# Thirteen gathers of a graph layer fetched row by row by SyncE instead of by GpSimd's indirect DMA

## The chip, the core and the metric

The kernel runs on one core of a Trainium2 chip. Its five engines (TensorE for products, VectorE and ScalarE for elementwise work, GpSimd, and SyncE, which here only issues transfers) run side by side and wait for one another through semaphores. Transfers between the memory of the chip (HBM) and the core's working memory are issued by SyncE or GpSimd and carried by 16 transfer engines. The metric is the device time of one execution in microseconds; less is better.

## The reference

One residual block around two graph convolutions, N = 6250 nodes, E = 100000 edges sorted by destination, D = 512, all float32:

```python
def reference(x, src, dst, W1_0, W1_1, b1, gamma, beta, W2_0, W2_1, b2):
    h = relu(layernorm(x))
    deg  = segment_sum(1, src);  dinv = where(deg > 0, rsqrt(deg), 0)
    norm = -dinv[src] * dinv[dst]
    prop = lambda h: segment_sum(h[src] * norm[:, None], dst)
    t = h @ W1_0 + prop(h) @ W1_1 + b1
    t = layernorm(t) * gamma + beta;  t = where(t >= 0, t, 0.01 * t)
    return x + t @ W2_0 + prop(t) @ W2_1 + b2
```

So each of the two layers fetches, for each of 100000 edges, one row of 2 KB of a table and adds it to the row of the edge's destination.

## The kernel before

**Chunks and gathers.** The edges are cut into NC = 782 chunks of P = 128. For chunk t one `indirect_dma_start` on GpSimd (L250, L480, L490) fetches the 128 table rows named by column t of `sidx`, one row to each partition. The first 76 chunks of layer 0 (RAW) are fetched from `x` itself and are put through the layer norm in place; the later ones come from `tab[0]`, whose rows of W = 528 numbers carry the node's `dinv` in column 512 (so the rows need scaling after the gather), and in layer 1 from `tab[1]`, whose rows of 512 are already scaled. Layer 1's first 27 chunks (L490) are fetched before the last blocks of `tab[1]` are written, with the late rows held out and added by other means.

**Where the rows lie.** `places` is a buffer of 63 slots of 128 x 528 numbers. `slot(k)` gives the slot of chunk k (k counts on through layer 1): a ring of R = 55 slots, and in a first round also the 8 slots behind them. `lent` lends the weights' buffers to the first 12 chunks. From the middle of layer 0 on, the last 8 slots hold the second layer's weights (`w_late`, loaded by L896). `gather_to` (L473 to L483) issues gathers up to 55 chunks ahead of what has been summed.

**Groups of sums.** Three chunks are a unit, four units a group: NS = 66 groups a layer, 12 chunks each but for the first. `choose` (L589) builds on VectorE the matrices `sel` (128 edges x 32 nodes) that say which edge belongs to which node; `scale` (L636) multiplies them in layer 0 by the `dinv` column of the gathered rows (L647); `sums` (L652) multiplies them on TensorE with the rows (L660), and ScalarE copies the sum to `agg` (L673). The last chunk of a group is the last product of its sums.

**Blocks.** The 49 blocks of 128 nodes follow the groups. When all groups that reach into block i are summed, `turn` (L781) loads the block's own rows (`load_h`, L545; in layer 1 also `load_x`, L564), `place` (L685) moves the sums to their nodes (L693), `first_half` and `second` multiply with the two weights (L568), and `finish` (L746) adds the bias. In layer 0 it also does the layer norm, and SyncE stores the block twice: to `tab[1]` (L777, from `t`) and, after ScalarE and VectorE have made `g` (L779, L780; a single buffer), to `h_tab` (L782). In layer 1 SyncE stores the output (L757).

**Order.** The queues of TensorE, GpSimd and SyncE are in the order in which the program is written; VectorE's and ScalarE's are ordered by the framework's scheduler, by its own estimate of times. The loop over groups is at the end of `usual_path`: for each g it calls `gather_to`, finishes blocks, chooses, scales and sums. SyncE's transfers take eight semaphores in turn, so that a transfer also waits until the one eight places before it has landed. `general_path` runs only where the input is not of the expected form, which it is here.

Of the kernel before, what the change touches and what calls it, by code (L numbers as in the profile page):

```python
# [9 lines left out]
F32 = mybir.dt.float32  # L10
BF = mybir.dt.bfloat16
I32 = mybir.dt.int32
AF = mybir.ActivationFunctionType
OP = mybir.AluOpType
AX = mybir.AxisListType
# [3 lines left out]
SP = mybir.EngineType.SP  # L19

P = 128
# [4 lines left out]
Q = 32  # L26
NQ = P // Q
STEP = 3
DRIFT = 32
RE = 14  # L30
RAW = 76
PAD = 16
LATE = 3
AHEAD_OF = 27
JOIN = 12


def parts(r):
# [5 lines left out]
def gnn_kernel(  # L44
# [33 lines left out]
    nc = tc.nc  # L78
    N, D = x.shape
# [6 lines left out]
    NC = -(-E // P)  # L86
# [16 lines left out]
    tab = [dram.tile([n, w], F32, name=f"tab{i}") for i, (n, w) in enumerate(((NB * P, W), (N + 1, D)))]  # L103
    zero_row = (NB - LATE) * P
# [26 lines left out]
    pick = const.tile([P, P], BF, name="pick")  # L131
    src_lo = const.tile([P, P], BF, name="src_lo")
    src_hi = const.tile([P, RAW], F32, name="src_hi")
    p_id = const.tile([P, 1], F32, name="p_id")

# [288 lines left out]
    n_unseen = usual_path(tc, locals())  # L424
    stay.close()
    with tc.If(n_unseen > 0):
        general_path(tc, x, src, dst, bias1, bias2, gam, bet, w_sb, (W2_1, W2_0), dinv, ndinv, ident, iota_r,
                     eps, out)


def usual_path(tc, have):
    nc = tc.nc
    (x, out, tab, h_tab, ndinv, sidx, dlx, iota_r, w_sb, W2_1, W2_0, w_late, ident, eps, ones, first, nodes_ps, node_of, minus,
     unsorted, dinv, sdinv, bias1, bias2, gam, bet, unseen, unit, N, E, D, NB, NC, NU, NS, KD, rows, places, R,
     load_rest, sc, pick, src_lo, src_hi, eidx, e_src, zero_row, p_id, lent, X) = (
        have[n] for n in ("x out tab h_tab ndinv sidx dlx iota_r w_sb W2_1 W2_0 w_late ident eps ones first nodes_ps node_of "
                          "minus unsorted dinv sdinv bias1 bias2 gam bet unseen unit N E D NB NC NU NS KD rows places "
                          "R load_rest sc pick src_lo src_hi eidx e_src zero_row p_id lent X").split())
# [12 lines left out]
    with ExitStack() as es:  # L451
# [11 lines left out]

        LATER = places.shape[1] - R

        def slot(k):
            return k - X if k < X + R + LATER else (k - X - LATER) % R

        def zr(layer, t):
            k = layer * NC + t  # L470
            return lent[k] if k < X else places[:, slot(k), :D]

        def gather_to(layer, summed_to):  # L473
            nonlocal gathered
            end = summed_to + R
            if layer == 0:
                end = max(end, min(end + LATER, X + LATER + 2 * R))
            for t in range(gathered, min(end, NC)):
                own_scale = layer == 0 and t >= RAW
                nc.gpsimd.indirect_dma_start(  # L480
                    out=places[:, slot(t), :] if own_scale else zr(layer, t), out_offset=None,
                    in_=x if layer == 0 and t < RAW else tab[layer],
                    in_offset=bass.IndirectOffsetOnAxis(  # L483
                        ap=lidx[:, t - SHIFTED : t - SHIFTED + 1] if layer and t >= SHIFTED else sidx[:, t : t + 1], axis=0))
            gathered = max(gathered, min(end, NC))
# [149 lines left out]
        def scale(sel, chunk, of=(0, NQ)):  # L635

            at = chunk[0][0]
            start = max(chunk[of[0]][0], RAW)
            end = chunk[min(of[1], len(chunk)) - 1][-1] + 1
            if end <= start:  # L640
                return
            each = sel.rearrange("p q s e -> p (q s) e")
            cut = sorted({start, end} | {t for t in range(start + 1, end) if slot(t) != slot(t - 1) + 1})
            for lo, hi in zip(cut, cut[1:]):
                v = each[:, lo - at : hi - at, :]
                k = slot(lo)
                last = nc.vector.tensor_tensor(  # L647
                    v, v, places[:, k : k + hi - lo, D : D + 1].to_broadcast([P, hi - lo, Q]), op=OP.mult)
            return last

        def sums(layer, g, sel, chunk, cnt=None, some=None, opens=True, closes=True):

            n = len(chunk)
            if opens:
                summed[0] = psum.tile([P, D], F32, name="ps")
            ps = summed[0]
            if some is None:
                some = [(s, q) for s in range(STEP) for q in range(n) if s < len(chunk[q])]
            for s, q in some:
                nc.tensor.matmul(ps[q * Q : (q + 1) * Q, :], sel[:, q, s, :], zr(layer, chunk[q][s]), start=(s == 0),  # L660
                                 stop=(s == len(chunk[q]) - 1 and (cnt is None or chunk[q][0] >= AHEAD_OF)))
# [224 lines left out]
        for layer in range(2):  # L886
# [5 lines left out]
            for g in range(NS - 1):  # L892
                gather_to(layer, STEP * unit[g])
                if layer == 0 and g == NS // 2:
                    for k, w in enumerate((W2_1, W2_0)):
                        nc.sync.dma_start(w_late[:, k], w.rearrange("(k p) d -> p k d", p=P))  # L896
                if layer == 0:
                    look_up("hT_ps")
                    find("hT_ps")
                    assert looked >= min(RAW, STEP * unit[g + 1])  # L900
                due = []

                def finished():
# [17 lines left out]
                sel, chunk = chosen.pop(g) if g in chosen else choose(g)  # L921
                if layer == 0:
# [103 lines left out]
    return n_unseen  # L1026


def general_path(tc, x, src, dst, bias1, bias2, gam, bet, w_sb, w_late, dinv, ndinv, ident, iota_r, eps,
                 out):  # L1030


# [31 lines left out]
    z_tab = [dram.tile([N, D], F32, name=f"z_tab{i}") for i in range(2)]  # L1064
    e_src = dram.tile([NC, P], I32, name="e_src")
    e_dst = dram.tile([NC, P], I32, name="e_dst")
    w_sb = list(w_sb)
    for k, w in enumerate(w_late):
        w_sb.append(const.tile([P, KD, D], F32, name=f"w_late{k}"))
# [284 lines left out]
```

## Time and profile before

| | us |
|---|---|
| three timed runs, median (lowest to highest) | 2020.21 (2019.19 to 2025.29) |
| the profiled execution, its own time | 2021.09 |
| its span in the trace | 2019.3 |
| TensorE busy | 1669.7 (83%) |
| GpSimd busy | 1488.9 (74%) |
| VectorE busy | 707.6 (35%) |
| ScalarE busy | 414.3 (21%) |

The durations come from the one profiled execution, whose own time is 0.9 us above the median of the timed runs. A share of busy time is an average over the whole span; issuing of transfers by SyncE isn't counted as busy. SyncE's transfer issues are listed as SPq.

### The profile page before, as it was taken

What the parts mean: (1) busy time and instruction counts of PE and PEld (TensorE: products, weight loads), DVE (VectorE), ACT (ScalarE), POOL (GpSimd) and SP (SyncE); (2) the same over time, 40 slices, a digit from 0 to 9 for tenths busy, and PEclk for the clock granted to TensorE, in tenths of its full rate; (3) what the DMA queues carried; (4) which work ended last, traced back from release to release, by engine and by line L of the source; (5) the groups of instructions that cost most, each with busy time, mean ns of one, the idle gap of its engine ahead of it and who ended that gap; (6) DMA issues with size and microseconds to landing.
All of it is one profiled execution on the core that took longest, in us unless ns stands there. A gap on an engine that the chain in (4) does not pass through costs nothing.

```text
span 2019.3 us, 20097 instructions
## 1 busy us (share of the span) xinstructions
PE 1669.7 (83%) x6907; PEld 669.5 (33%) x6907; DVE 707.6 (35%) x1498; ACT 414.3 (21%) x752; POOL 1488.9 (74%) x1578
## 2 busy tenths in 40 slices
PE   5579998776887776888879888888888888888988
PEld 4444443222333222333323322323332223333333
DVE  7975554333354334343363111112221212222211
ACT  7895221111121111121111010011010001011100
POOL 6477777777777777777777777777777777777774
PEclk8789999888998888989999998889999989989999
DMA  9998888888988888888887787788787878788875
GB/s 329 396 374 269 267 269 263 249 258 245 303 265 253 251 260 241 267 266 260 245 261 241 245 257 247 247 252 255 240 255 246 254 244 257 241 263 251 272 235 171
DMA packets 190131, 528.41 MB, mean 262 GB/s; under 512 B 34652, under 2 KB 36426, under 8 KB 190020
## 3 DMA queue, kind: packets, MB, share of 16 engines
q0 software_dynamic: 125120, 415.88, 67.7%
q1 hardware_dynamic: 64860, 111.14, 15.2%
q8 instruction: 56, 0.92, 0.2%
q14 instruction: 55, 0.45, 0.1%
q10 hardware_dynamic: 40, 0.02, 0.0%
HBM read 475.25 MB, written 51.66 MB: 261 GB/s over the span
## 4 chain that ended last, share of the span: by engine, by line
PE 39%; DMA 31%; POOL 12%; issue 10%; DVE 5%; ACT 2%; POOLq 0%; DVEq 0%; SPq 0%; ACTq 0%
DMA places<-tab,sidx 24%; PE u_ps L568 16%; POOL places L480 12%; PE ps L660 12%; PE an_ps L693 7%; DMA places<-tab,lidx 5%; PE hT_ps L556 1%; PE hT_ps L803 1%; DVE hi L362 1%; DVE lo L362 1%; ACT places L539 1%; DMA dst_c<-in_dst_dram 1%; DMA tab<-places 1%; PE both_ps L379 1%; DVE sel L647 0%
## 5 line engine op out<-in xcount | busy, mean ns | idle before, releaser
L480 POOL DMA_INDIRECT places<-tab,sidx x1191 | 1130.5, 949 | 363.4 <-issue 256.2
L660 PE MATMUL ps<-places,sel 128*32 128x512 f32 x3104 | 517.1, 671 | 145.4 <-DMA places<-tab,sidx 81.9
L693 PE MATMUL an_ps<-agg,there 128*128 128x512 f32 (+1 forms) x554 | 270.0, 620 | 88.2 <-ACT agg L673 83.2
L480 POOL DMA_INDIRECT places<-tab,lidx x270 | 255.3, 946 | 82.3 <-issue 60.9
L660 PEld LDWEIGHTS ps<-places,sel 128*32 128x32 f32 x3104 | 103.1, 117 | 524.1 <-issue 190.0
L607 DVE TENSOR_TENSOR sel<-dlx,nodes_ps 128x384 f32<-128x384 f32 (+3 forms) x134 | 72.4, 541 | 415.1 <-PE ps L660 415.1
L568 PE MATMUL u_ps<-w,hT 128*128 128x512 f32 (+1 forms) x400 | 185.3, 607 | 20.6 <-ACT hT L558 20.1
L673 ACT ACTIVATE agg<-ps 128x512 f32<-128x512 f32 (+2 forms) x130 | 76.1, 587 | 570.1 <-PE ps L660 545.1
L568 PE MATMUL u_ps<-places,hT 128*128 128x512 f32 (+2 forms) x408 | 182.4, 591 | 2.9 <-ACT hT L558 2.9
L568 PE MATMUL u_ps<-w,aT 128*128 128x512 f32 x384 | 173.2, 594 | 2.7 <-DVE aT L805 2.7
L693 PEld LDWEIGHTS an_ps<-agg,there 128*128 128x128 f32 (+1 forms) x554 | 105.8, 199 | 209.6 <-issue 109.8
L568 PE MATMUL u_ps<-places,aT 128*128 128x512 f32 x384 | 173.5, 594 | 0.8 <-DVE aT L805 0.8
L647 DVE TENSOR_TENSOR sel<-sel,places 128x384 f32<-128x384 f32 (+11 forms) x71 | 34.4, 490 | 328.3 <-DMA places<-tab,sidx 323.2
L754 DVE TENSOR_TENSOR u_ps<-u_ps,bias 128x512 f32<-128x512 f32 x45 | 31.5, 700 | 281.8 <-PE u_ps L568 281.8
L558 ACT ACTIVATE hT<-hT_ps 128x512 f32<-128x512 f32 (+1 forms) x98 | 58.2, 594 | 278.1 <-PE hT_ps L556 277.6
L796 ACT ACTIVATE an<-an_ps,ndinv 128x512 f32<-128x512 f32 x96 | 65.8, 685 | 213.7 <-PE an_ps L693 213.5
L681 DVE TENSOR_SCALAR there<-iota_r,node_of 128x128 f32<-128x128 f32 (+1 forms) x286 | 85.8, 302 | 63.6 <-PE an_ps L693 61.3
L568 PEld LDWEIGHTS u_ps<-w,hT 128*128 128x128 f32 (+1 forms) x400 | 73.7, 195 | 96.5 <-issue 74.7
L766 ACT ACTIVATE sd<-mv,eps 128x1 f32<-128x1 f32 (+1 forms) x49 | 14.4, 294 | 433.5 <-DVE mv L764 433.5
L250 POOL DMA_INDIRECT places<-in_x_dram,sidx x63 | 60.0, 952 | 54.0 <-ACT junk L266 21.1
L568 PEld LDWEIGHTS u_ps<-places,hT 128*128 128x128 f32 (+1 forms) x408 | 74.4, 192 | 76.5 <-issue 71.5
L568 PEld LDWEIGHTS u_ps<-w,aT 128*128 128x128 f32 x384 | 70.7, 190 | 83.0 <-issue 77.8
(197 smaller groups left out, 1318.6 us busy)
## 6 DMA issues: line engine op xcount, KB each, us to landing
places<-tab,sidx POOLq DMA_INDIRECT x1191, 3.8
h_tab<-g SPq DMA_DIRECT2D x48, 256.0 KB
xt<-in_x_dram SPq DMA_DIRECT2D x48, 256.0 KB
out_dram<-t SPq DMA_DIRECT2D x48, 256.0 KB
tab<-t SPq DMA_DIRECT2D x46, 256.0 KB
tab<-places SPq DMA_DIRECT2D x22, 528.0 KB
h<-tab SPq DMA_DIRECT2D x45, 256.0 KB
h<-h_tab SPq DMA_DIRECT2D x45, 256.0 KB
```

Source lines behind the costliest of these rows:

```text
L250: nc.gpsimd.indirect_dma_start(out=lent[t] if t < X else places[:, t - X, :D], out_offset=None, in_=x, in_offset=bass.IndirectOffsetOnAxis ...
L362: nc.vector.tensor_tensor(t, s[:, g * 2 * GJ : (g + 1) * 2 * GJ].rearrange("p (j s) -> p j s", s=2)[:, :, None, :] .to_broadcast([EP, GJ, ...
L480: nc.gpsimd.indirect_dma_start(out=places[:, slot(t), :] if own_scale else zr(layer, t), out_offset=None, in_=x if layer == 0 and t < RAW ...
L558: nc.scalar.activation(hT[:, :, :r], ps[:, :, :r], AF.Copy)
L568: nc.tensor.matmul(u_ps[:r], hT[:, kc, :r], w[:, kc, :], start=(start and kc == 0), stop=(stop and kc == KD - 1))
L607: nc.vector.tensor_tensor(sel[:, q : q + k, :w, :], of, node[:, q : q + k, None, :].to_broadcast([P, k, w, Q]), op=OP.is_equal)
L647: last = nc.vector.tensor_tensor(v, v, places[:, k : k + hi - lo, D : D + 1].to_broadcast([P, hi - lo, Q]), op=OP.mult)
L660: nc.tensor.matmul(ps[q * Q : (q + 1) * Q, :], sel[:, q, s, :], zr(layer, chunk[q][s]), start=(s == 0), stop=(s == len(chunk[q]) - 1 and ( ...
L673: nc.scalar.activation(agg[g][: n * Q, lo : lo + w], ps[: n * Q, lo : lo + w], AF.Copy)
L681: behind[1] = nc.vector.tensor_scalar(t[:m, :r], iota_r[:m, :r], node_of[:m, g : g + 1], -(1.0 + i * P), op0=OP.subtract, op1=OP.is_equal)
L693: nc.tensor.matmul(placed[i][:r], t[:m, :r], agg[g][:m, :], start=(g == inside[i][0]), stop=(g == inside[i][-1]))
L796: nc.scalar.activation(an[:r], placed.pop(i)[:r], AF.Copy, scale=ndinv[:r, i : i + 1])
```

## The change

Six chunks of layer 0 (the last chunk of groups 17, 25, 33, 41, 49 and 57) and seven of layer 1 (of groups 12, 20, 28, 36, 44, 52 and 60) are no longer gathered by GpSimd. SyncE fetches their 128 rows one by one: each row is one transfer from the table at an address held in a register, in 16 pieces of 128 B (132 B in layer 0, so that the last piece brings column 512 along), written with gaps to 16 places of one partition. From group 7 in layer 0 and group 2 in layer 1 on, 8 rows are issued ahead of a group's work and 8 behind it; a chunk takes eight groups, and is summed two groups after the one that issued its last rows. The rows go to two slots of `places` in turn (the slots that held `W2_1`'s first half, whose load moves from group 33 to group 62), in layer 1 to the buffer of `W1_0`. The byte addresses are set up in group 6 by two loads of `src` and eight VectorE operations, in the memory of `pick` and `src_lo`, which are done by then; SyncE loads eight of them into registers ahead of each run of eight rows. Products with such a chunk read 16 pieces of 32 numbers; `scale` takes its chunk apart from its neighbours. `general_path` loads the first layer's weights again.

```diff
+AT_ONCE = 8
+PIECES = (16, 16)
+ONE_BY_ONE = (7, 2)
+SECOND = 32
...
+        for layer, g in enumerate(ONE_BY_ONE):
+            for j in range(SECOND):
+                at = g + -(-P * (j + 1) // (2 * AT_ONCE)) + 2
+                if at > NS - 5:
+                    break
+                t = STEP * unit[at + 1] - 1
+                one_by_one[layer * NC + t] = (layer * SECOND + j, R + j % 2 if layer == 0 else j % 2)
...
+        def set_starts():
+            for layer, some in enumerate(own_rows):
...
+                at, up = (pool.tile([P, D], F32, name="xt")[rows_of, :P] for _ in range(2))
+                nc.sync.dma_start(starts[rows_of], bass.AP(tensor=src.tensor, offset=src.offset + some[0] * P,
+                                                           ap=[[step * P, n], [1, P]]))
+                nc.vector.tensor_copy(at, starts[rows_of])
+                if layer:
+                    nc.vector.tensor_single_scalar(up, at, float(zero_row), op=OP.is_ge)
+                    nc.vector.tensor_add(at, at, up)
+                nc.vector.tensor_scalar_mul(at, at, 4.0 * tab[layer].shape[1])
+                nc.vector.tensor_copy(starts[rows_of], at)
...
+        def fetch(layer):
+            some = to_fetch[:AT_ONCE]
+            del to_fetch[:AT_ONCE]
+            for t in sorted({t for t, _ in some}):
+                fetch_rows(layer, t, [e for of, e in some if of == t])
+
+        def fetch_rows(layer, t, es):
...
+            _, regs = nc.values_load_multi_w_load_instructions(
+                starts[at : at + 1, e : e + n], engines=(SP,), ...)
+            flat = tab[layer].bitcast(U8).rearrange("n d -> (n d)")
+            w = PIECE[layer] + 1 - layer
+            flat = bass.AP(tensor=flat.tensor, offset=flat.offset,
+                           ap=[[1, flat.shape[0]], [PIECE[layer] * 4, PIECES[layer]], [1, w * 4]])
+            to = spread(layer * NC + t)[:, :, :w].bitcast(U8)
+            for j, start in enumerate(regs):
+                nc.sync.dma_start(to[e + j : e + j + 1], flat[bass.ds(start, 1)])
...
             for t in range(gathered, min(end, NC)):
+                if layer * NC + t in one_by_one:
+                    continue
...
                 if layer == 0 and g == NS // 2:
-                    for k, w in enumerate((W2_1, W2_0)):
-                        nc.sync.dma_start(w_late[:, k], w.rearrange("(k p) d -> p k d", p=P))
+                    nc.sync.dma_start(w_late[:, 1], W2_0.rearrange("(k p) d -> p k d", p=P))
+                if layer == 0 and g == NS - 4:
+                    nc.sync.dma_start(w_late[:, 0], W2_1.rearrange("(k p) d -> p k d", p=P))
...
+                if layer == 0 and g == ONE_BY_ONE[0] - 1:
+                    set_starts()
+                if g == ONE_BY_ONE[layer]:
+                    to_fetch.extend((t, e) for t in own_rows[layer] for e in range(P))
+                fetch(layer)
...
+                fetch(layer)
```

The first `fetch` of a group stands behind `gather_to` and ahead of the blocks' work, the second behind the group's sums.

More of the change, by code (lines that the diff above doesn't have):

```diff
@@ L12 @@
 I32 = mybir.dt.int32
+U8 = mybir.dt.uint8
 AF = mybir.ActivationFunctionType
@@ L130, in gnn_kernel @@
     sc = const.tile([P, 2, NB], F32, name="sc")
-    pick = const.tile([P, P], BF, name="pick")
-    src_lo = const.tile([P, P], BF, name="src_lo")
+    low_of = const.tile([P, 2, P], BF, name="low_of")
+    pick, src_lo = (low_of[:, k, :] for k in range(2))
+    starts = low_of.rearrange("p k e -> p (k e)").bitcast(I32)
     src_hi = const.tile([P, RAW], F32, name="src_hi")
@@ L464, in usual_path @@
         LATER = places.shape[1] - R
+        one_by_one, to_fetch = {}, []
+        for layer, g in enumerate(ONE_BY_ONE):
[5 more added lines that the diff above has]
+                one_by_one[layer * NC + t] = (layer * SECOND + j, R + j % 2 if layer == 0 else j % 2)
+        own_rows = [sorted(k - layer * NC for k in one_by_one if k // NC == layer) for layer in range(2)]
@@ new lines, in set_starts @@
+        def set_starts():
+            for layer, some in enumerate(own_rows):
+                n, step = len(some), some[1] - some[0]
+                assert some == [some[0] + j * step for j in range(n)]
+                rows_of = slice(layer * SECOND, layer * SECOND + n)
+                at, up = (pool.tile([P, D], F32, name="xt")[rows_of, :P] for _ in range(2))
[7 more added lines that the diff above has]
+                nc.vector.tensor_copy(starts[rows_of], at)
@@ new lines, in usual_path, with spread @@
+        PIECE = [D // k for k in PIECES]
+        w_free = w_sb[1].rearrange("p k d -> p (k d)")
+        def spread(k):
+            at = one_by_one[k][1]
+            row = places[:, at, :] if k < NC else w_free[:, at * W : (at + 1) * W]
+            return row.rearrange("p (a b) -> p a b", a=PIECES[k // NC])
+        def fetch(layer):
[3 more added lines that the diff above has]
+                fetch_rows(layer, t, [e for of, e in some if of == t])
@@ new lines, in fetch_rows @@
+        def fetch_rows(layer, t, es):
+            e, n = es[0], len(es)
+            at = one_by_one[layer * NC + t][0]
+            _, regs = nc.values_load_multi_w_load_instructions(
+                starts[at : at + 1, e : e + n], engines=(SP,), min_val=0, max_val=(tab[layer].shape[0] - 1) * tab[layer].shape[1] * 4,
+                skip_runtime_bounds_check_because="rows of the table")
+            flat = tab[layer].bitcast(U8).rearrange("n d -> (n d)")
[5 more added lines that the diff above has]
+                nc.sync.dma_start(to[e + j : e + j + 1], flat[bass.ds(start, 1)])
@@ L470, in zr @@
             k = layer * NC + t
+            if k in one_by_one:
+                return spread(k)[:, :, : PIECE[layer]]
             return lent[k] if k < X else places[:, slot(k), :D]
@@ L642, in scale @@
             each = sel.rearrange("p q s e -> p (q s) e")
-            cut = sorted({start, end} | {t for t in range(start + 1, end) if slot(t) != slot(t - 1) + 1})
+            cut = sorted({start, end} | {t for t in range(start + 1, end) if slot(t) != slot(t - 1) + 1
+                                         or t in one_by_one or t - 1 in one_by_one})
             for lo, hi in zip(cut, cut[1:]):
@@ L659, in sums @@
             for s, q in some:
-                nc.tensor.matmul(ps[q * Q : (q + 1) * Q, :], sel[:, q, s, :], zr(layer, chunk[q][s]), start=(s == 0),
+                rows_of = zr(layer, chunk[q][s])
+                to = ps[q * Q : (q + 1) * Q, :]
+                if len(rows_of.shape) > 2:
+                    to = to.rearrange("p (a b) -> p a b", a=PIECES[layer])
+                nc.tensor.matmul(to, sel[:, q, s, :], rows_of, start=(s == 0),
                                  stop=(s == len(chunk[q]) - 1 and (cnt is None or chunk[q][0] >= AHEAD_OF)))
@@ L921, in usual_path @@
                 sel, chunk = chosen.pop(g) if g in chosen else choose(g)
+                assert not any(t in own_rows[layer] and to_fetch and t >= to_fetch[0][0] for c in chunk for t in c)
                 if layer == 0:
```

18 lines of the change are left out of this document (13 added, 5 removed).

## The prediction, made before the changed kernel ran

> **What bounds the kernel now.** I read the page's busy shares and chain of waits first, then GpSimd's groups, its instructions in order of time, its waits, and the table by stretches of the span.
>
> ```profile
> span 2019.3 us, 20097 instructions
> ...
> PE 1669.7 (83%) x6907; PEld 669.5 (33%) x6907; DVE 707.6 (35%) x1498; ACT 414.3 (21%) x752; POOL 1488.9 (74%) x1578
> ...
> PE 39%; DMA 31%; POOL 12%; issue 10%; DVE 5%; ACT 2%; POOLq 0%; DVEq 0%; SPq 0%; ACTq 0%
> ```
>
> By busy share TensorE (83%) looks like the bound and GpSimd (74%) has room. The groups and the order of time say otherwise:
>
> ```profile
> L480 POOL DMA_INDIRECT places<-tab,sidx x1191 | 1130.5, 949 | 363.4 <-issue 256.2 <-DMA places<-tab,sidx 66.7 <-PE ps L660 15.2
> L480 POOL DMA_INDIRECT places<-tab,lidx x270 | 255.3, 946 | 82.3 <-issue 60.9 <-DMA places<-tab,lidx 13.7 <-PE ps L660 3.0
> ...
> L490 POOL DMA_INDIRECT places<-tab,eidx x27 | 26.9, 997 | 8.2 <-issue 5.2 <-DMA places<-tab,eidx 1.8 <-DMA h_tab<-g 0.3
> ```
>
> ```profile
> 134.92 0.95 POOL L480 DMA_INDIRECT places<-tab,sidx  x1 [0.30 <-issue]
> 136.17 0.94 POOL L480 DMA_INDIRECT places<-tab,sidx  x1 [0.30 <-issue]
> ...
> 2000.31 0.95 POOL L480 DMA_INDIRECT places<-tab,lidx  x1 [0.30 <-issue]
> ```
>
> ```profile
> POOL places L480 <- issue: 316.5, 1039, 0.3
> POOL places L480 <- DMA places<-tab,sidx: 66.7, 219, 0.3
> ```
>
> From 134.92 to 2000.31 us lie 1191 + 270 + 27 = 1488 gathers of table rows, so 1487 intervals over 1865.39 us: 1.2545 us from one to the next, 0.95 busy and 0.30 of "idle" that is never longer (the last number of the waits is the longest). No buffer, engine or transfer holds GpSimd back in these 1865 us; it issues as fast as it can, and the busy share hides it because the 0.30 us isn't counted. TensorE has time left beside it:
>
> ```profile
> 335.00:1000.00 665.00, 527.48 (x2114) 206.88 (x2112) 257.58 (x584) 116.23 (x213) 503.50 (x531) 0.89 0.84 259
> 1100.00:1950.00 850.00, 736.00 (x2693) 266.47 (x2691) 175.84 (x379) 91.52 (x147) 643.07 (x680) 0.94 0.81 252
> ```
>
> (Columns: stretch, length, PE, PEld, DVE, ACT, POOL, clock, DMA share, GB/s.) TensorE is busy 79% in layer 0 and 87% in layer 1: 11.9 and 13.0 us of a group of sums that lasts 12 x 1.2545 = 15.05 us. The end of the chain:
>
> ```profile
> 1971.55 5.51 DMA places<-tab,lidx
> 1977.11 1.04 PE ps L660 x2
> ...
> 2008.13 4.35 PE u_ps L568 x18
> 2012.50 0.42 DVE t L738
> ```
>
> The last wait for a gather ends at 1977; the rest is TensorE's own tail. The change ends its fetches several groups before that (layer 1's last is summed in group 60 of 66), so this tail moves as a whole.
>
> **What goes.** 6 + 7 = 13 of the 1488 gathers leave GpSimd's queue, and nothing else in that queue changes: 13 x 1.2545 = 16.3 us. They leave before the tail and, in layer 0, before the layer's end, so each makes all later gathers earlier. TensorE needs to follow by 1.25 us in one group of eight; its 2.0 us of slack in every group of layer 1 (15.05 - 13.0) and 3.1 in layer 0 cover it.
>
> **What comes: SyncE's rows.** 13 x 128 = 1664 transfers of one row, each in 16 pieces of 128 or 132 B, in runs of 8 behind one load of 8 registers. They ride on the same eight semaphores in rotation as SyncE's other transfers, so each row also waits for the transfer issued eight places earlier to land. No run shows a row of this form; the nearest rows:
>
> ```profile
> 4.62 0.25 SPq L168 DMA_DIRECT2D src_c<-in_src_dram  x1
> ...
> L545 SPq DMA_DIRECT2D h<-tab x45: 319/320/1032, 131.1 to 949.4; - x45
> ...
> L740 SPq TENSOR_LOAD <-unseen x1: 538/538/538, 2011.6 to 2011.6; - x1
> ```
>
> ```profile
> 0.74 0.41 SPq L160 DMA_DIRECT2D src_c<-in_src_dram  x1
> ...
> 2.54 0.23 DVE L236 CAST f<-src_c 128x128 f32<-128x128 int32 x1 [1.06 <-DMA src_c<-in_src_dram]
> ...
> 1043.81 4.87 DMA h_tab<-g
> ...
> DMA to landing us min/median/max: 3.4/3.9/7.8
> ```
>
> Issue alone: 0.25 us (a transfer of one partition) to 0.32 us (128 rows); I take 0.37 with the gap between two. Landing: 1.8 us in the quiet start (issue 0.74, used 2.54), 4.87 us for a store under load, 3.9 median and 7.8 longest for a gather; divided by eight, 0.23, 0.61, 0.49 and 0.98 us per row. I take 0.5 us, nearest to the 3.9 us median: per group 16 x 0.5 + 2 x 0.54 (register loads) = 9.1 us, and three loads and stores for each of 49 blocks in 66 groups, 2.2 x 0.37 = 0.8 us. SyncE then works 9.9 us of a group of (12 - 1/8) x 1.2545 = 14.9 us. It keeps pace as long as a row costs under (14.9 - 1.1 - 0.8) / 16 = 0.81 us. A chunk is summed with two whole groups between its last row and its sum, so some 30 us of lateness cost nothing.
>
> **What queues behind the rows.** SyncE's queue is in order: a block's load and stores stand behind up to 16 rows, and rows behind a store that waits for VectorE. In the built order VectorE's `g`, which the second store needs, has also moved behind the scaling of the next group's matrices, which waits for gathers:
>
> ```profile
> 584.13 0.69 DVE L780 TENSOR_TENSOR g<-u_ps,g 128x512 f32<-128x512 f32 x1 [0.20 <-ACT g L779]
> ...
> 590.50 0.56 DVE L647 TENSOR_TENSOR sel<-sel,places 128x384 f32<-128x384 f32 x1 [5.08 <-issue]
> ...
> 584.85 0.32 SPq L782 DMA_DIRECT2D h_tab<-g  x1
> ...
> 596.22 0.32 SPq L777 DMA_DIRECT2D tab<-t  x1
> ```
>
> The store of 584.85 would go out near 592, 9 us of rows end near 601, and the next block's first store, ready at 596.2, goes about 5 us late. The table store is needed only at the layer's end; the `g` buffer is single, and its next write comes about a group later, after a landing of 4.87 us. I cost this at nothing in layer 0, where TensorE's 3.1 us per group cover it; without cover it costs what it overruns.
>
> **Setting up the row addresses**, in group 6. TensorE is behind there, and one place is tight:
>
> ```profile
> 201.42 0.94 POOL L480 DMA_INDIRECT places<-tab,sidx  x1 [0.30 <-issue]
> 203.25 0.94 POOL L480 DMA_INDIRECT places<-tab,sidx  x1 [0.88 <-DVE u_ps L770]
> ...
> 192.72 0.29 DVE L596 TENSOR_TENSOR nodes_ps<-nodes_ps,iota_r 128x128 f32<-128x128 f32 x1
> 198.99 0.70 DVE L760 TENSOR_TENSOR u_ps<-u_ps,bias 128x512 f32<-128x512 f32 x1 [5.97 <-PE u_ps L568]
> ```
>
> The gather of 203.25 waited for group 7's sums to free its slot, so a delay of TensorE there would pass to GpSimd one for one. The eight new VectorE operations come between 192 and 199 in the built order, about 8 x 0.25 = 2 us inside an idle time of 5.97 us: nothing, up to 3 us if the index load lands late.
>
> **The layer's end.** Layer 1's first gather from the whole table (the 28th) needs the last table store:
>
> ```profile
> 1047.07 0.73 SPq L777 DMA_DIRECT2D tab<-pre  x2
> ...
> 1056.87 0.94 POOL L480 DMA_INDIRECT places<-tab,sidx  x1 [0.30 <-issue]
> ```
>
> With a landing of 4.87 us it is there near 1052.7, 4 us to spare, and both sides move together. The weight load moved to group 62 is one issue. The 13 sums read rows with gaps and wait on eight semaphores at the last product of a group, where TensorE waits anyway; the six extra scalings are under 0.5 us each. Nothing.
>
> **Sum.** 2020.21 - 16.3 = 2003.9 us. The profiled execution took 2021.09 (span 2019.3), 0.9 above the median, and should come near 2004.8.
>
> **Rivals.** (1) *SyncE cannot keep up.* Above 0.81 us a row its queue sets the pace. At 0.98 (landings as long as the longest gather's) a group lasts 16 x 0.98 + 1.9 = 17.6 us: 2.7 more in 104 groups, less the 30 us of slack in each layer and the 16.3 saved: about 2225 us. For it: no row of this form is in the trace. Against: all three typical rows lie below 0.61. Chance 0.11. The Trainium skill (DMA: Bandwidth & Descriptors, Rules for kernel authors) speaks against many small transfers: under 64 KB one pays mostly overhead. Its section on the anatomy of one DMA puts the fixed part at about 2 us, for GpSimd's path; paid one after another that would be, as an estimate from the page, 32 us a group, with eight in flight 4. No run here shows which holds for these rows.
>
> (2) *The transfer engines fill up.*
>
> ```profile
> q0 software_dynamic: 125120, 415.88, 67.7%
> q1 hardware_dynamic: 64860, 111.14, 15.2%
> ...
> 100.00:135.00 35.00, 25.38 (x181) 17.18 (x181) 29.70 (x76) 34.23 (x50) 25.15 (x28) 0.83 1.05 366
> ```
>
> The hardware queue's packets, mostly 2 KB, took 0.152 x 16 x 2019.3 / 64860 = 76 ns each. A row adds 16 pieces and 16 semaphore writes, two packets per engine: at 76 ns a group adds 16 x 2 x 0.076 = 2.4 us, 16%, to a share of 0.81 to 0.84, about full. It decides from 84 ns (0.18 x 14.9 / 32). At the software queue's 175 ns (0.677 x 16 x 2019.3 / 125120) the group would last 0.82 x 14.9 + 5.6 = 17.8 us, about +300 us less what is saved. Against: pieces a sixteenth as large should be well under 76 ns, and with the engines full between 100 and 135 us GpSimd still issued 28 gathers in 35 us, 1.25 each. Chance 0.07. The Trainium skill (DMA: Bandwidth & Descriptors, Specifications) puts line rate at 512 B and more and has shorter transfers read, modify and write, which speaks for this rival; the trace of before has no such data pieces.
>
> (3) *The saving is given back in part*, by late stores that hold ScalarE's `g`, or the tight place at 203 us: 6 us and more of the 16.3, 2010 to 2020. Chance 0.10, half of it on either side of 2014.
>
> **How the numbers follow.** The measurement of this kernel can tell about 0.3%, 6 us, from no change: 2014 to 2026 is "same". Forecast 0.72, at 2004 with 2001 to 2010 for late landings and the spread of the runs. Faster: 0.72 + 0.05 = 0.77; same: 0.05 + 0.01; slower: 0.17. The range takes in the forecast's own and rival 3's, 2000 to 2020.
>
> **What would show it.** Right: 1475 table gathers still 1.25 us apart with no longer wait, GpSimd's last issue near 1984, TensorE's tail as before. Rival 1: row transfers over 0.8 us apart and sums waiting for `tab` rows from the hardware queue. Rival 2: a transfer share near 1.0 and landings well over 3.9 us. Wrong altogether: GpSimd waiting in mid-layer, or its interval above 1.27 us.

## The result: about 15 us faster, and the profile after

| | before | changed kernel | ratio (95% interval) |
|---|---|---|---|
| first measurement, medians of 6 runs each | 2019.7 us | 2008.41 us (2003.02 to 2011.45) | 0.9931 (0.9908 to 0.9954) |
| repeated, 6 runs against 21 | 2021.9 us | 2006.40 us (2004.94 to 2008.77) | 0.9924 (0.9913 to 0.9936) |
| profiled execution, own time (span) | 2021.09 us (2019.3) | 2003.02 us (2001.1) | |

The gain is 9 to 19 us by the first interval and 13 to 18 by the second; by the medians it is 11.3 and 15.5 us. All the kernels below but one ran where the kernel before took 2021 to 2022 us; the one with 26 rows ran on a chip that gave 2459 us for the kernel before as well, and its time is not set beside the others'.

The page of the changed kernel (busy time and share by engine, then the chain that ended last, then the hardware queue's row):

```profile
span 2001.1 us, 23764 instructions
...
PE 1664.2 (83%) x6907; PEld 677.2 (34%) x6907; DVE 715.4 (36%) x1512; ACT 415.5 (21%) x752; POOL 1476.8 (74%) x1565
...
q1 hardware_dynamic: 118134, 114.71, 17.7%
...
PE 38%; DMA 20%; SPq 15%; issue 10%; POOL 8%; DVE 7%; ACT 2%; POOLq 0%; DVEq 0%; ACTq 0%
```

The shares of the engines are what they were; new is SyncE's queue (SPq) with 15% of the chain. GpSimd in order of time, first and last gather of a table row, and its longest groups of waits (total us, times, longest us):

```profile
133.29 0.95 POOL L550 DMA_INDIRECT places<-tab,sidx  x1 [0.30 <-issue]
...
1982.66 0.95 POOL L550 DMA_INDIRECT places<-tab,lidx  x1 [0.30 <-issue]
```

```profile
POOL places L550 <- issue: 320.8, 1053, 0.3
POOL places L550 <- DMA places<-tab,sidx: 58.8, 193, 0.3
...
POOL places L560 <- issue: 7.2, 21, 1.1
```

From 133.29 to 1982.66 lie 1475 gathers, 1474 intervals of 1.2547 us, where 1487 intervals of 1.2545 lay before. No wait is longer than 0.3 us but one of 1.1. The span is 18.2 us shorter: 16.0 between the first and the last gather, 1.6 because the first came earlier (133.29 for 134.92), 0.6 in the tail behind the last (18.4 for 19.0). The start varies from one execution to the next and is not put down to the change: in the repeated run of the same kernel the first table gather came at 136.98 and the span was 2004.9. There the stretch from first to last gather was 15.3 us shorter than before.

The one wait of 1.1 us is at the layer's end, at the first of the 27 gathers of layer 1 that go ahead. That gather reads `tab[1]`, so it needs the last store from `t`; a VectorE operation that writes `t` anew waits for the same store and shows when it landed. First before, then the changed kernel:

```profile
1020.54 0.56 DVE L624 TENSOR_TENSOR t<-e_src,iota_r 128x384 bf16<-128x384 f32 x1 [2.92 <-DMA tab<-t]
...
1021.72 0.95 POOL L490 DMA_INDIRECT places<-tab,eidx  x1 [0.30 <-DMA h_tab<-g]
```

```profile
1011.89 0.56 DVE L694 TENSOR_TENSOR t<-e_src,iota_r 128x384 bf16<-128x384 f32 x1 [3.04 <-DMA tab<-t]
...
1012.55 0.94 POOL L560 DMA_INDIRECT places<-tab,eidx  x1 [1.15 <-issue]
```

Before, the gather was issued 1.2 us after that store had landed, without a longer wait than usual; in the changed kernel 0.7 us after it, late by 0.8. So this place had about half a microsecond to spare before the change, and it is where lateness in layer 0 first costs time.

TensorE's waits of before (first line) and of the changed kernel (the other two), and its two stretches (length, PE, PEld, DVE, ACT, POOL, clock, DMA share, GB/s):

```profile
PE an_ps L693 <- ACT agg L673: 83.2, 8, 13.6
```

```profile
PE hT_ps L626 <- DMA h<-tab: 90.9, 12, 11.7
...
PE hT_ps L626 <- DMA h<-h_tab: 24.3, 12, 3.4
```

```profile
335.00:1000.00 665.00, 544.42 (x2189) 219.41 (x2182) 267.07 (x601) 122.29 (x221) 503.42 (x531) 0.91 0.86 264
...
1100.00:1950.00 850.00, 731.62 (x2695) 267.87 (x2695) 174.72 (x377) 90.92 (x146) 643.01 (x680) 0.93 0.82 254
```

TensorE's slack is spent in another place: it now waits for a block's own rows `h`, whose load stands behind rows in SyncE's queue. That costs no time as long as GpSimd's gathers don't wait, and they don't. Now that queue, in order of time, with the row transfers and the register loads by themselves (min/median/max ns), and its waits between 400 and 800 us, first of before, then of the changed kernel:

```profile
656.70 0.52 SPq L615 DMA_DIRECT2D h<-tab  x1
657.31 0.38 SPq L853 DMA_DIRECT2D tab<-t  x1
657.79 0.38 SPq L858 DMA_DIRECT2D h_tab<-g  x1
659.98 10.60 SPq L527 DMA_DIRECT2D places<-tab  x16
670.67 0.53 SPq L615 DMA_DIRECT2D h<-tab  x1
```

```profile
L527 SPq DMA_DIRECT2D places<-tab x768: 506/537/1345, 194.6 to 890.7; - x192
...
L518 SPq TENSOR_LOAD <-low_of x1: 533/533/533, 644.5 to 644.5; - x1
...
L518 SPq TENSOR_LOAD <-low_of x1: 1647/1647/1647, 658.2 to 658.2; - x1
```

```profile
SPq L777 <- DVE t L774: 176.6, 16, 26.5
SPq L777 <- DVE there L681: 82.5, 3, 27.8
SPq L545 <- PE hT_ps L556: 53.9, 13, 6.7
```

```profile
SPq L858 <- DVE g L856: 16.7, 4, 6.5
SPq L858 <- DVE there L757: 15.0, 5, 10.5
```

Before, SyncE spent over 300 of these 400 us waiting for a block to be ready. Now it waits for some 42 in all; the rest is issue and register loads. Its queue is nine tenths full.

### The profile page after: what moved, and what is told of

The parts are those of the page before. It is cut to its first block, busy times and chain, and to the rows that moved or that the text cites. A ratio compares the mean times of both kernels' runs of the same rounds, so it can differ in the third digit from the quotient of the medians.

```text
span 2001.1 us, 23764 instructions
## 1 busy us (share of the span) xinstructions
PE 1664.2 (83%) x6907; PEld 677.2 (34%) x6907; DVE 715.4 (36%) x1512; ACT 415.5 (21%) x752; POOL 1476.8 (74%) x1565
## 3 DMA queue, kind: packets, MB, share of 16 engines
q1 hardware_dynamic: 118134, 114.71, 17.7%
## 4 chain that ended last, share of the span: by engine, by line
PE 38%; DMA 20%; SPq 15%; issue 10%; POOL 8%; DVE 7%; ACT 2%; POOLq 0%; DVEq 0%; ACTq 0%
PE u_ps L638 18%; SPq L527 12%; PE ps L736 11%; DMA places<-tab,sidx 8%; POOL places L550 8%; PE an_ps L769 5%; DMA places<-tab,lidx 3%; DMA h<-tab 2%; DMA h<-h_tab 2%; SPq L518 2%; PE hT_ps L626 2%; PE hT_ps L879 1%; DVE hi L368 1%; DVE lo L368 1%; DMA w<-in_L_gnn_W_dram 1%
## 5 line engine op out<-in xcount | busy, mean ns | idle before, releaser
L736 PE MATMUL ps<-places,sel 128*32 128x512 f32 x3090 | 485.1, 640 | 95.0 <-DMA places<-tab,sidx 65.6
L769 PE MATMUL an_ps<-agg,there 128*128 128x512 f32 (+1 forms) x554 | 257.2, 598 | 5.9 <-ACT agg L749 4.3
L638 PE MATMUL u_ps<-w,aT 128*128 128x512 f32 x384 | 193.7, 652 | 2.5 <-DVE aT L881 2.5
L638 PE MATMUL u_ps<-places,aT 128*128 128x512 f32 x384 | 178.9, 609 | 0.8 <-DVE aT L881 0.8
L626 PE MATMUL hT_ps<-ident,h 128*128 128x128 f32 x360 | 63.1, 303 | 115.1 <-DMA h<-tab 90.9
L830 DVE TENSOR_TENSOR u_ps<-u_ps,bias 128x512 f32<-128x512 f32 x45 | 31.5, 699 | 258.3 <-PE u_ps L638 252.5
L836 DVE TENSOR_TENSOR u_ps<-u_ps,bias 128x512 f32<-128x512 f32 x45 | 31.4, 698 | 235.2 <-PE u_ps L638 235.2
L638 PEld LDWEIGHTS u_ps<-w,aT 128*128 128x128 f32 x384 | 79.5, 214 | 96.1 <-issue 92.1
L626 PEld LDWEIGHTS hT_ps<-ident,h 128*128 128x128 f32 x360 | 45.3, 153 | 177.5 <-issue 164.1
```

Of the source, the lines that this page charges most:

```text
L626: nc.tensor.transpose(ps[:, kc, :r], h[:r, kc * P : (kc + 1) * P], ident[:r, :r])
L638: nc.tensor.matmul(u_ps[:r], hT[:, kc, :r], w[:, kc, :], start=(start and kc == 0), stop=(stop and kc == KD - 1))
L736: nc.tensor.matmul(to, sel[:, q, s, :], rows_of, start=(s == 0), stop=(s == len(chunk[q]) - 1 and (cnt is None or chunk[q][0] >= AHEAD_OF)))
L769: nc.tensor.matmul(placed[i][:r], t[:m, :r], agg[g][:m, :], start=(g == inside[i][0]), stop=(g == inside[i][-1]))
```

## The experiments

Each edit is against the changed kernel. GpSimd's interval is written i = 1.2545 us. Three questions were put: does each chunk taken off bring one i, what do the rows cost, and where does that end?

**Nothing changed, and no rows at all.** The repeat:

> The changed kernel unchanged, so that the others have it on the same chip. Theory A (GpSimd's queue is the bound and SyncE's rows are hidden): 13 x 1.2545 = 16.3 us faster than before, ratio 0.992, gathers 1.25 us apart from end to end. Theory B (the rows give part of the saving back through SyncE's queue, by block loads that come late to TensorE): 10 to 14 us faster, ratio 0.993 to 0.995, and in a profiled execution TensorE waits for h loads.

```diff
-            _, regs = nc.values_load_multi_w_load_instructions(...)
+            regs = []
```

> The 13 chunks are gathered by nobody: SyncE neither loads the addresses nor fetches the rows (the sums read what lies in the buffers; 13 chunks are left out of the result), everything else is as changed. This is the saving without its price. Theory A: as the changed kernel, 16.3 us under before, within 1 us of e1. Theory B: 2 to 6 us under e1. Rival (transfer engines fill up): also under e1, and the share of the transfer engines falls back to 0.81 to 0.84 from 0.86.

Measured: 2006.40 us (0.9924, 0.9913 to 0.9936) with the rows and 2006.17 us (0.9923, 0.9909 to 0.9937) without any. The 1664 transfers and 208 register loads cost nothing that can be measured. Without them TensorE waits as it did before:

```profile
PE an_ps L767 <- ACT agg L747: 83.4, 8, 13.8
```

**The rows beside all the gathers.** Rows are fetched, but no product reads them, and GpSimd gathers all 1488 chunks.

```diff
-                if layer * NC + t in one_by_one:
-                    continue
```

> SyncE fetches the 1664 rows as in the changed kernel, but GpSimd gathers all chunks as before and the sums use its gathers; nobody reads the rows. This is the price without the saving. Theory A: as before, within 2 us. Theory B: 2 to 6 us slower than before, since TensorE waits for late h loads as in the changed kernel. If the rows slowed GpSimd's own issue, the gathers would be more than 1.25 us apart.

Measured: 2023.51 us, ratio 1.0003 (0.9994 to 1.0013). The rows and the moved weight load are free, with TensorE's new wait there in full:

```profile
PE hT_ps L619 <- DMA h<-tab: 96.0, 12, 11.9
```

By the interval the rows cost at most 2.6 us, so the gain comes from what left GpSimd's queue.

**Half as many rows.**

```diff
-AT_ONCE = 8
+AT_ONCE = 4
```

> The changed kernel with 8 rows a group (runs of 4) instead of 16, so that a chunk takes 16 groups and only 3 + 3 chunks leave GpSimd. SyncE is busy with rows for about 6 us of a group. If a chunk is worth one GpSimd interval (theory A): 6 x 1.2545 = 7.5 us under before, ratio 0.9963, half of what 13 chunks gave. If SyncE's load costs something at 16 rows a group (theory B), a chunk is worth more here than there: over 8 us.

Measured: 2013.83 us, ratio 0.9961 (0.9947 to 0.9975): 7.5 us less than the kernel before beside it (2021.35), and 6 x i is 7.5. The interval, 5 to 11 us, doesn't by itself tell this from the "over 8 us" of theory B.

**Taking the wait for `h` away.** A third buffer lets its load go out one block earlier; in the program the load now stands behind the transposes of the block in hand, where it stood ahead of them.

```diff
+            if i % 3 == 0 and (layer or i >= 10):
+                own_h[i] = w_sb[0]... if layer else places[:, R + 2, :D]
...
-            if i + AHEAD < NB:
-                load(layer, i + AHEAD)
...
+            while load_to[0] < min(NB - 1, i + (AHEAD + 1 if layer or i >= 8 else AHEAD)):
+                load_to[0] += 1
+                load(layer, load_to[0])
```

> The changed kernel with a third buffer for the blocks' own rows (a free slot of places in layer 0 from block 10 on, the first weight buffer in layer 1), so that these loads are issued three blocks ahead instead of two. Theory A: as e1, within 1 us, though TensorE's waits for h loads (115 us in the profile of the changed kernel) go. Theory B: these waits are where the saving went, so 2 to 6 us under e1.

Measured: 2029.03 us, ratio 1.0032 (1.0021 to 1.0044), 22 us above the changed kernel, which neither theory has. The waits for `h` are down to 13.6 us, another is there, and GpSimd stops once, at the layer's end:

```profile
PE u_ps L644 <- DVE g L862: 90.5, 24, 8.3
```

```profile
1015.68 0.95 POOL L550 DMA_INDIRECT places<-tab,sidx  x1 [0.30 <-issue]
1038.54 0.94 POOL L560 DMA_INDIRECT places<-tab,eidx  x1 [21.91 <-DMA tab<-t]
```

The one gap of 21.9 us is about the whole loss, and it is at the tight place shown above: TensorE ran late through layer 0, and the last table store with it. I thought that VectorE's place for `g`, behind the scaling, was to blame, and forced the scaling behind `g`:

```diff
-            nc.vector.tensor_tensor(g[:r], v, g[:r], op=OP.max)
+            behind[3] = nc.vector.tensor_tensor(g[:r], v, g[:r], op=OP.max)
```

> As e4 (third buffer for the blocks' own rows), with VectorE's scaling of a group held behind the g of the block finished before it, as it stands in the kernel before. Theory: e4 lost 22 us because VectorE's g stood behind the scaling, so TensorE waited 90 us for the sums' buffer that g reads, layer 0 ended late, and GpSimd waited 21.9 us for the last table stores. Then this has no such wait and takes 15 to 17 us less than before, as e1. If the third buffer itself is the cause, it stays 5 to 10 us over before.

Measured: 2143.66 us, ratio 1.0605 (1.0589 to 1.0621). The forecast fails, but it doesn't settle the theory: the wait for `g` is gone, and the forced order brought a larger one. Now the sums wait for the scaling, and GpSimd for the sums.

```profile
PE ps L742 <- DVE sel L725: 208.2, 41, 6.8
```

Why the third buffer costs time stays open. What both runs show is that the changed kernel has little room left around the last table store and `g`.

**More rows in 16 pieces.** 22 rows a group, a chunk every six groups, 17 chunks (the same filling up of a chunk's last run, by `range(132)`, is in all kernels with a length of group given by hand).

```diff
-AT_ONCE = 8
+AT_ONCE = 11
...
-                at = g + -(-P * (j + 1) // (2 * AT_ONCE)) + 2
+                at = g + 6 * (j + 1) + 2
```

> The changed kernel with up to 22 rows a group (runs of 11) and a chunk every six groups, so that 8 + 9 = 17 chunks leave GpSimd. If SyncE had room: 17 x 1.2545 = 21.3 us under before, ratio 0.9895. By the issue time of a row in the profile of the changed kernel (0.537 + 0.029 us and a gap, 0.63 together) SyncE needs 128 / 6 x 0.63 + 2 x 0.53 + 0.8 = 15.3 us of rows, register loads and other transfers in a group of (12 - 1/6) x 1.2545 = 14.8 us, without its waits: rival 1 of the prediction should show, rows late for the sums, and the time above the changed kernel's, 0 to 60 us slower than it. A threshold of 0.81 us a row at 16 rows is 13.0 us of row time a group; here it is 13.4.

Measured: 2488.26 us, ratio 1.2315 (1.2293 to 1.2336): 467 us slower than the kernel before, far outside what any theory expected. GpSimd waits for sums:

```profile
POOL places L550 <- PE ps L736: 469.8, 95, 26.0
...
POOL places L560 <- DMA tab<-t: 18.4, 1, 18.4
```

These two are the most of it: 459 us beyond the usual 0.3 us of each, of the 488 that were lost (467 and the 21 that 17 chunks should bring). SyncE in order of time, its register loads between 465 and 500 us, and its longest wait between 400 and 800:

```profile
468.43 0.38 SPq L858 DMA_DIRECT2D h_tab<-g  x1
473.02 14.99 SPq L527 DMA_DIRECT2D places<-tab  x22
488.05 0.57 SPq L853 DMA_DIRECT2D tab<-t  x1
488.72 0.38 SPq L858 DMA_DIRECT2D h_tab<-g  x1
492.85 16.47 SPq L527 DMA_DIRECT2D places<-tab  x22
```

```profile
L518 SPq TENSOR_LOAD <-low_of x3: 1154/3593/4044, 468.9 to 489.1; - x3
```

```profile
SPq L527 <- DMA places<-in_L_gnn_W_dram: 2.0, 1, 2.0
```

The four microseconds between a store and the next row look like a wait and are none: a load of 11 registers took 4.04 us at 468.9 and 3.59 at 489.1 (8 registers took 0.53, or 1.65 behind stores). So SyncE is never idle here, and needs 19.8 us (473.02 to 492.85) for a group that GpSimd could do in (12 - 1/6) x i = 14.8. Over all groups it is much the same: 20.4 us in the 48 groups of layer 0 that fetch rows and 19.6 in the 54 of layer 1, with 9 and 13 us of waits in all. TensorE waits for `h` behind it, and everything for TensorE:

```profile
PE hT_ps L626 <- DMA h<-h_tab: 343.4, 30, 24.3
PE hT_ps L626 <- DMA h<-tab: 330.4, 22, 25.9
```

What the groups take over 14.8 us makes 520 us in the 102 groups; 488 were lost. The granted clock of TensorE was lower, 0.83 against 0.92, but its busy time was not longer (1646.0 us against 1664.2).

The lengths of the register loads have a pattern that the edit brought in unseen. Behind a row, a load of 11 took 1.15 to 1.18 us when it began at an edge number divisible by four (0, 44 and 88 of a chunk's 128; 46 loads) and 2.26 to 2.33 us at the others (49 loads); behind stores it took up to 4.35. The changed kernel's loads of 8 all begin at such numbers. So a part of this loss, about 1.1 us in three loads of four, belongs to the length of 11 and not to more rows. Without it a group would still take some 18 us.

**The same in one piece.** A row in one piece adds 2 packets to the hardware queue instead of 32 (68214 packets in all against 118134, and 64886 without rows). First with the 13 chunks:

```diff
-PIECES = (16, 16)
+PIECES = (1, 1)
```

> The changed kernel with each row in one piece of 2 KB instead of 16 of 128 B: one transfer engine per row. If the issue time of a row (0.54 us) is spent on its 16 pieces, it falls to 0.25 to 0.35 us; if it belongs to a transfer with a register address, it stays at 0.54. Theory A: the time stays as e1 (about 16 us under before) either way, as long as the rows land two groups ahead of their sums. If all rows go to the same engine, 16 x 2 KB a group on top of its share of the gathers may hold the gathers back: then later gathers land late and the time is over the changed kernel's.

Measured: 2007.29 us, ratio 0.9926 (0.9910 to 0.9941), the changed kernel's time; but a row's issue fell from 537 to 228 ns, SyncE has idle time again (294 of the 695 us of layer 0's rows), and TensorE waits little for `h` (25.3 us):

```profile
L527 SPq DMA_DIRECT2D places<-tab x768: 227/228/543, 192.8 to 887.1; - x192
```

> The changed kernel with each row in 4 pieces of 512 B. Issue time of a row between that of one piece and 0.54 us if pieces cost; the added packets fall from 53274 to about a quarter. Theory A: the time of e1, about 16 us under before. Four engines carry all rows, so a smaller unevenness than with one piece.

With 4 pieces: 2009.52 us, ratio 0.9947 (0.9930 to 0.9963). That is 11.8 us under before where about 16 were expected. Four pieces cost more to issue than sixteen, 577 ns, and here SyncE is just full. Its rows in layer 0, its longest group of waits between 400 and 800 us, and GpSimd's one long gap:

```profile
L527 SPq DMA_DIRECT2D places<-tab x768: 576/577/775, 196.3 to 917.0; - x192
```

```profile
SPq L858 <- DVE there L757: 2.2, 3, 1.4
```

```profile
1021.24 0.94 POOL L560 DMA_INDIRECT places<-tab,eidx  x1 [4.71 <-issue]
```

The 48 groups of rows take (917.0 - 196.3) / 48 = 15.0 us each, against 14.9 of GpSimd's; the lateness that gathers, some 6 us, shows at the layer's end, at the same tight place.

**22 rows in one piece**, 17 chunks: the two edits together.

> As e6 (22 rows a group, 8 + 9 = 17 chunks off GpSimd), but each row in one piece, whose issue took 0.228 + 0.029 us in e7 against 0.537 + 0.029. SyncE needs about 128 / 6 x 0.32 + 2 x 0.53 + 0.8 = 8.7 us a group of 14.8. If SyncE's time per group is what broke e6 (467 us slower), this has no such loss: 17 x 1.2545 = 21.3 us under before, about 2000 us. If the number of rows in flight or landed was the trouble, it stays far above before.

Measured: 2001.16 us (2000.06 to 2005.47), ratio 0.9905 (0.9888 to 0.9923), 20.4 us below the kernel before beside it; 17 x i is 21.3. Against the 22 rows in 16 pieces only the pieces changed, and 487 us went. With them the packets became fewer too, but the transfer engines weren't full in the run with 16 pieces (their share was 0.64 from 335 to 1000 us and 0.73 from 1100 to 1950), so it is the issue that counts. This is the fastest kernel of the study; its interval still touches the changed kernel's (0.9913 to 0.9936). The register loads (here those between 400 and 800 us) are as long as with 16 pieces, and SyncE is nearly full, but the group fits:

```profile
L518 SPq TENSOR_LOAD <-low_of x55: 1364/2534/4371, 402.1 to 789.4; - x55
```

**32 rows in one piece**, 27 chunks (`AT_ONCE = 16`).

> 32 rows a group (runs of 16) of one piece each, a chunk every four groups: 13 + 14 = 27 chunks off GpSimd, 33.9 us under before, about 1987 us, if SyncE keeps pace: 32 x 0.32 + 2 x 0.53 + 0.8 = 12.1 us of a group of 11.75 x 1.2545 = 14.7, as much as the changed kernel's 16 rows of 16 pieces (12 us). TensorE's busy 13.0 us of a group in layer 1 still fits. Rival: TensorE waits for late block loads and the gain stays under 25 us; or one transfer engine, which carries all rows, fills up and gathers land late.

Measured: 2155.28 us, ratio 1.0658 (1.0639 to 1.0677), a miss: 134 us slower than before where 34 were to be gained. SyncE in order of time, then GpSimd's wait for sums and TensorE's for `h`:

```profile
499.75 0.38 SPq L858 DMA_DIRECT2D h_tab<-g  x1
502.67 12.62 SPq L527 DMA_DIRECT2D places<-tab  x32
515.40 0.36 SPq L615 DMA_DIRECT2D h<-tab  x1
517.09 2.83 SPq L527 DMA_DIRECT2D places<-tab  x8
```

```profile
POOL places L550 <- PE ps L736: 135.9, 78, 12.0
```

```profile
PE hT_ps L626 <- DMA h<-h_tab: 210.3, 21, 19.3
PE hT_ps L626 <- DMA h<-tab: 199.2, 17, 20.3
```

12.6 us of rows with one load of 16 registers inside, another of 2.4 us ahead of them, and the block's transfers: some 16 us for a group of (12 - 1/4) x i = 14.7. Over all groups it is 16.3 us in layer 0 and 16.7 in layer 1, of which 1.3 and 2.2 are waits, so the queue's own work, 15.0 and 14.5, is about the whole group and its waits no longer fit. Some of these are new: rows 0.33 us apart wait for the row eight places earlier to land, 59 us in all. The first rival is what came, late block loads, at a far higher price than it had; the second isn't, since TensorE waited only 12.4 us in all for gathers named by `sidx` (65.6 in the changed kernel), and the transfer engines' share fell to 0.80.

**26 rows in one piece, registers loaded by 8 and 5**, 21 chunks, to see whether shorter loads move the limit.

```diff
-                fetch_rows(layer, t, [e for of, e in some if of == t])
+                es = [e for of, e in some if of == t]
+                for k in range(0, len(es), 8):
+                    fetch_rows(layer, t, es[k : k + 8])
```

> 21 chunks, 26 rows a group in one piece each, the registers loaded by 8 and by 5 in place of 11, 13 or 16 at once. Theory A: what decides is whether SyncE's queue, counted with its register loads, fits into a group of (12 - 1/5) x 1.2545 = 14.8 us; loads of up to 8 registers are short (0.53 us in the changed kernel, where loads of 11 took 2.5 us in the run with 22 rows). 26 x 0.33 + 4 x 0.7 + 1.3 = 12.7 us: it fits, and 21 x 1.2545 = 26.3 us come off: 1995 us, ratio 0.987, register loads under 1 us on the mean. Theory B: a load takes 2.5 us whenever SyncE's queue is as full as this, whatever its size: 26 x 0.33 + 4 x 2.5 + 1.3 = 19.9 us a group, some 5 us over in 100 groups, near 2500 us. Theory C: the rows' landings set a limit of their own above 22 rows a group: rows further apart than 0.33 us, loads short, time between the two.

Measured: 2928.19 us beside 2458.95 for the kernel before, ratio 1.1919 (1.1867 to 1.1971). It is inconclusive, since there even the kernel before was 22% slower than beside every other run. The register loads show the pattern of the 22 rows again: behind rows, 8 registers took 0.79 us (median) from an edge number divisible by four and 1.92 from the others. Runs of 13 begin mostly at the others, so neither theory A nor B had the loads right; whether the kernel would fit elsewhere stays open.

## Why the prediction was right, point by point

- **What bounds the kernel.** Right, though "never longer" had an exception in its own lines, the 0.88 us at 203.25. GpSimd's interval stayed at 1.2547 us, and the time follows the number of chunks taken off it: 6, 13 and 17 chunks brought 7.5, 15.5 and 20.4 us, where the interval gives 7.5, 16.3 and 21.3. The last issue came at 1982.66 (1984 forecast), and the tail moved as a whole.
- **The rows at nothing.** Right in what it costs, and shown from both sides (no rows: the same time; rows beside all gathers: the time of before). The cover was thinner than the sum had it. SyncE was put at 9.9 us of a 14.9 us group and takes 13.0 in layer 0 and 12.7 in layer 1 (from first row to last, less its waits), and 14.0 in the group with a block's stores shown above. Three terms were mis-sized. A row takes 0.63 us from one to the next (10.60 us for 16 with a register load of 0.53 among them), not 0.5, and what sets it is the issue of 537 ns with the setting of its address, not an eighth of a landing. That the landing's eighth came near is luck: the prediction's own figure for issue, 0.37 with the gap, would have been far too low. A register load takes 0.53 us, as put, but behind a block's store to `h_tab` 0.92 at the median and up to 2.1. A block's `h` load behind rows takes 0.53, not 0.37.
- **The limit at 0.81 us a row.** Too high: the loads and the block's transfers take 13.0 - 16 x 0.63 = 2.9 us of a group on the mean, not 1.9, and it is (14.9 - 2.9) / 16 = 0.75. It isn't a fixed limit either. The run with 4 pieces reached it with 0.67 us a row, because its register loads were longer too (behind rows 1.05 us instead of 0.53).
- **Late stores and late loads.** Right that they come, and that layer 0's slack covers them. The load of `h` was named as standing behind the rows, but only the stores were priced; it became TensorE's longest wait, 115 us in all, at no cost here. At the layer's end the prediction looked at the wrong gather: the 28th, with 4 us to spare, waited 0.3 us as ever, while the first of the 27 ahead of it, with half a microsecond, was 0.8 us late. The runs that lost time at the layer's end lost it there: 21.9 us with the third buffer, 18.4 with 22 rows in 16 pieces, 4.7 with 4 pieces.
- **Row addresses in group 6, the 13 sums, the weight load.** Nothing, as forecast: no gather there waited over 0.3 us.
- **Rival 1, SyncE cannot keep up.** It did not decide, but it is the rival that was near: six more rows a group in 16 pieces made it true, at +467 us. Its condition was put as landings; it is issue. The Trainium skill (DMA: Bandwidth & Descriptors, Rules for kernel authors) says that many small transfers mostly pay overhead. These runs agree for the issuing queue, 0.63 us for each 2 KB. The wait for landing isn't part of it with eight in flight and rows 0.63 us apart (between 400 and 800 us no row waited for another row); at 0.33 us apart, in the runs of one piece with 22 and 32 rows, it begins to be, with 32 and 59 us in all.
- **Rival 2, the transfer engines fill.** Not so. The 53274 packets added to the hardware queue took (0.177 x 2001.1 - 0.152 x 2019.3) x 16 / 53274 = 14 ns each, a fifth of the 76 taken as a bound, and the share of the transfer engines went from 0.84 to 0.86 in layer 0. Taken one by one, a piece of 128 B took 12.8 ns on the mean, one of 132 B 16.1 and a semaphore write 9.4, beside 91.5 for 2 KB. The prediction overlooked that the trace of before has small pieces too: two of 128 B, at 13 ns, and the store of `dinv` in pieces of 4 B. The Trainium skill (DMA: Bandwidth & Descriptors, Specifications) has transfers under 512 B read, modify and write; what these pieces paid for it is within their 12.8 and 16.1 ns.
- **Rival 3, a part given back.** At most a little: 15.5 us of 16.3 in the repeated measurement, with the difference inside its interval. The first measurement, by its medians, has 11.3; its six runs spread over 8 us, and its interval too takes in 16.3. The times, 2008.41 and 2006.40, lie 4.5 and 2.5 us above the 2003.9 forecast. What is missing isn't shown to come from the rows, since the kernel without any took 2006.17.

## What to carry to other kernels

An engine whose idle times are all equal and never longer was the bound here, at a busy share of 74%: count its instructions, and price each one taken away at the interval. An in-order queue took moved work for free until it was full, and then every load and store behind it was late and the whole kernel went at that queue's pace; so sum the queue by issue, register loads and waits over one group, not by transfer time, before adding to it. A wait that vanished on the engine with slack came up elsewhere on it, and only a wait of the bounding engine counted; where that engine itself has to wait for something, as at the layer's end, look for the first place, not the last.

## What the runs showed of the chip that was not expected

- The issue of a transfer at an address from a register depends on its pieces, and not steadily: 228 ns in one piece, 577 in 4 (512 B), 537 in 16 (128 B).
- The time of a register load on SyncE goes with where it begins. Medians behind rows: for 11 registers 1.15 us from an edge number divisible by four and 2.27 from others (22 rows in 16 pieces); for 8 registers 0.79 and 1.92 (26 rows). The two sorts don't overlap in the run with 22 rows. No run varied the start alone.
- It goes with what stands ahead of it as well: 8 registers from such a number took 0.53 us behind rows of 16 pieces, 0.79 behind rows of one and 1.05 behind rows of 4, and up to 2.35 behind stores. Four registers took 0.30 us, 16 took 1.24. Such a load looks like idle time of the queue in a list of its transfers.
